# Norm factors in spare PSUM columns, a cross product read from the transform's bank, and a residual added on GpSimd, in the last phases of a two-layer kernel

## The chip, the cores and the metric

The kernel runs on one core of a Trainium2 chip. The metric is the device time of one execution in microseconds (us), the median of several runs. The engines are called here as the profile calls them: PE is the matmul engine (its weight loads are PEld), DVE is VectorE, ACT is ScalarE, POOL is GpSimd, and SP is the engine whose queue issues the DMAs in this part. SBUF is the on-chip working memory, PSUM the memory that matmuls write.

## What is computed

There are two layers with residuals, `x = x + layer(group_norm(x))`. Layer 0, a state-space scan in four directions, takes most of the time and is not touched. Layer 1 is a Fourier neural operator with attention over time steps. Its attention is computed before the part that matters here, which is the reference's last lines:

```python
projd = _fno_layer(out, wP, wPs, bPs, (H, W))
attention = _inorm(projd + xa, norm_g[1], norm_b[1])
an = _inorm(attention, norm_g[2], norm_b[2])
m = _fno_layer(an, wM0, wM0s, bM0s, (H, W), (norm_g[3], norm_b[3]), act=True)
m = _fno_layer(m, wM1, wM1s, bM1s, (H, W), (norm_g[4], norm_b[4]), act=False)
output = _inorm(m, norm_g[5], norm_b[5]) + attention
```

`_inorm` subtracts an image's mean, and divides by its standard deviation. `_fno_layer` is a truncated Fourier transform, a product with complex weights, the transform back (this is normalized where `norm_gb` is given), plus a scaled copy of its input (the skip), and for M0 a GELU. There are 192 images (4 x 48) of 128 x 48 points, in float32.

## The kernel before

The last part of `layer1` works on two strands, one for each pair of batches (`class Strand`, `p` is 0 or 1). A strand holds 96 images side by side (P = 96). An image tensor is laid out as 128 partitions (the long axis) by 48 rows by 96 images; `self.y` is the attention output in `xa`, `self.m` the MLP image. A block is 4 rows (QB), 128 x 384 elements, and fills 384 of the 512 columns of a PSUM bank.

A strand runs six phases. Each is a main generator (`p0` to `p5`) and a tail (`t0` to `t5`): `p0` and `t0` transform the projection back along the rows, `p1` along the columns, with sums for the norm of y and the forward transform for M0 beside it; `t1` makes the factors of that norm. `p2` multiplies by M0's weights and transforms back along the rows, `t2` makes the factor `t3` of M0's norm, `p3` transforms back along the columns, adds the skip, applies GELU, and starts M1's forward transform. `t3_` finishes that. `p4` and `t4` do for M1 what `p2` and `t2` do for M0, and make the factors `qe` and `qm` and a bias. `p5` and `t5` finish and store the output.

The loop at the end of `layer1` takes the phases of both strands in turn: p0 of strand 0, p0 of strand 1, p1 of strand 0, and so on. Beside each main generator it advances the tail of the phase before it, two steps of the tail for each step of the main. So `t2` of strand 0 is recorded beside `p2` of strand 1, and `p5` of strand 0 beside `t4` of strand 1. Instructions recorded through `on` keep their recorded order on their engine, so that an instruction waits behind all that were recorded before it. DMAs through `nc.sync` may be placed by the scheduler, and each engine and SP's queue then runs in order.

The lines that the change and the steps of the prediction touch:

- `rsqrt` writes a square root with ACT into a small SBUF vector of 128 x 96, and takes the reciprocal of it with DVE in place. `times` is an ACT copy with a scale.
- `open_sums` takes a new PSUM tile `st` for a strand's sums at the start of p1 to p4; each strand's tile has one bank. `sums` fills columns 0 to 383 of it; `total` reduces these with DVE and adds across partitions with PE.
- `p2` has POOL compute `m = y * sw` beside it, six blocks of 128 x 768 for each strand. `p3` has POOL scale `y` by `s1` in place, six more for each strand.
- `t2` ends with `t3 = t3 * s2`, a DVE product of two SBUF vectors. `p3` multiplies each loaded spectrum block `e2` (128 x 768) by `t3`.
- `along_h`, used by p0, p2 and p4, multiplies with PE into a bank, copies the bank to the SBUF tile `e` with ACT, and for each second bank calls `more`, and writes `e` to DRAM; `load_e2` loads it again with the axes turned (four DMAs for each block).
- `product` squares `e` with ACT or, in p4, also multiplies it with `a2`, on DVE, both from SBUF (`ce1`, 96 x 768). `beside` in p4 loads the layer's input `xr` and has POOL add it to `y`, six blocks of 128 x 768 for each strand.
- `p5` has for each second step a DVE product `e2 * qe` (called grade below), and `skip`: for two blocks of 128 x 768 each `m = m * qm`, then `m = m + y`, all on DVE with SBUF operands. Each step then adds two PSUM banks to `m` on DVE. `put` transposes finished rows with PE, adds the bias with ACT, and stores by DMA; step t puts the rows of step t - 1.

Of the kernel before, what the change touches and what calls it, by code (L numbers as in the profile page):

```python
# [10 lines left out]
F32 = mybir.dt.float32  # L11
BF16 = mybir.dt.bfloat16
AF = mybir.ActivationFunctionType
# [968 lines left out]
def layer1(ctx, tc, io, x1_dram, out):  # L982
# [893 lines left out]
    class Strand:  # L1876


        def __init__(self, p):
            self.p = p  # L1880
            self.y = xa[:, :, p * P : p * P + P]
            self.m = None
            self.e2 = {}

        def bank(self, name):
            return psum.tile([128, 512], F32, tag="mm", name=f"{name}_{self.p}")

        def open_sums(self, name):
            self.st = psst.tile([128, 512], F32, tag=f"st{self.p}", name=f"st_{name}_{self.p}")

        def blk(self, tag, shape, name, bufs):
            return work.tile(shape, F32, tag=tag, name=f"{name}_{self.p}", bufs=bufs)
# [19 lines left out]
            self.tot = [b[:, i * P : i * P + P] for i in range(len(mats))]  # L1912
            yield

        def rsqrt(self, name, v, bias, scale=1.0):
            r = self.vector(name)
            on.scalar.activation(r, v, AF.Sqrt, bias=bias, scale=scale)
            on.vector.reciprocal(r, r)
            return r

        def times(self, dst, src, factor):
            on.scalar.activation(dst, src, AF.Copy, scale=factor)
# [23 lines left out]
                yield  # L1946


        def along_h(self, name, fill, more=None, beside=None):
            self.de = dram.tile([2, H, 32, P], F32, name=f"de_{name}_{self.p}")  # L1950
            self.wait = []
            for k in range(0, 32, 4):
                if k % 8 == 0:
                    e = self.blk(f"spectra{self.p}", [128, 8, P], f"e_{name}{k}", 3)[0:96]
                b = self.bank(f"pe_{name}{k}")
                fill(b, k)
                if len(self.wait) > 1:
                    self.sums(self.wait.pop(0))
                on.scalar.copy(e[:, k % 8 : k % 8 + 4], images(b[0:96]))
                if k % 8 == 4:  # L1960
                    if more:
# [6 lines left out]
        def product(self, e, other, k0, name):  # L1968
            t = self.blk("ap", [128, 8, P], f"{name}{k0}", 4)[0:96]
            if other is None:  # L1970
                on.scalar.activation(t, e, AF.Square)
            else:
                on.vector.tensor_mul(t, e, other)
# [52 lines left out]

        def p1(self):

            self.open_sums("y")
            self.parts = []  # L2030
            for t in range(6):
                made = self.along_w("p", t, lambda h: pair_t[self.p][0:96, h])
                if t in (2, 4):
                    self.sums(self.parts[:4])
                    self.parts = self.parts[4:]
                for i, (b, h) in enumerate(made):
                    v = self.y[:, h : h + QB]
                    on.vector.tensor_add(v, v, images(b))
                    sq = self.blk("sq", [128, QB, P], f"sqy{h}", 4)
                    on.scalar.activation(sq, v, AF.Square)  # L2040
                    self.parts.append((2 * (t % 2) + i, one_m, sq, t < 2, t >= 4))
                if t:
                    self.forward("m0", self.y, t - 1, on.scalar.copy)
                yield
# [20 lines left out]
        def p2(self):  # L2065

            self.m = imgs.tile([128, H, P], F32, tag=f"p{self.p}", name=f"m_{self.p}")
            self.open_sums("m0")

            def fill(b, k):  # L2070
                for i in range(4):
                    on.tensor.matmul(b[0:96, i * P : i * P + P], sp_m[0][:, k + i], self.a2[:, k + i], start=True, stop=True)

            def more(e, k0):
                n = k0 // 8
                t = self.product(e, None, k0, "sqe0")
                self.wait.append([(2 * (n % 2) + i, one_s[0:96], t[i], n < 2, n >= 2) for i in range(2)])

            def beside(i):
                if i < 6:  # L2080
                    q = 8 * (3 * (i % 2) + i // 2)
                    on.gpsimd.tensor_mul(self.m[:, q : q + 8], self.y[:, q : q + 8], over(self.sw, 8))

            yield from self.along_h("m0", fill, more, beside)

        def t2(self):
            yield from self.load_e2("m0")
            for w in self.wait:
                self.sums(w)
            yield  # L2090
            yield from self.total((g_all,), "m0")
            on.vector.tensor_mul(self.s22, self.s22, self.tot[0])
            self.t3 = self.rsqrt("t3", self.s22, eps)
            on.vector.tensor_mul(self.t3, self.t3, self.s2)
            yield

        def p3(self):

            self.open_sums("g")
# [38 lines left out]

        def p4(self):

            self.open_sums("m1")

            def fill(b, k):
                for i in range(4):
                    on.tensor.matmul(b[0:96, i * P : i * P + P], sp_m[1][:, k + i], self.a2[:, k + i], start=True, stop=True)

            def more(e, k0):
                ts = [self.product(e, None, k0, "sqe1"), self.product(e, self.a2[:, k0 : k0 + 8], k0, "ce1")]
                self.wait.append(
                    [(2 * n + i, one_s[0:96], ts[n][i], k0 == 0, k0 == 24) for n in range(2) for i in range(2)]  # L2150
                )
# [7 lines left out]
                    v = self.y[:, q : q + 8]  # L2159
                    on.gpsimd.tensor_add(v, v, xr)  # L2160

            yield from self.along_h("m1", fill, more, beside)

        def t4(self):
            yield from self.load_e2("m1")
# [5 lines left out]
            t4 = self.rsqrt("t4", v4, eps)  # L2171
            self.times(t4, t4, n_g[:, 4:5])
            yield
            v5, u = self.vector("v5"), self.vector("d")
            on.vector.tensor_mul(v5, t4, v4)
            on.vector.tensor_mul(u, t4, cv)
            on.vector.tensor_mul(v5, v5, t4)
            self.times(u, u, w2)
            on.vector.tensor_add(v5, v5, self.vm)
            on.vector.tensor_add(v5, v5, u)  # L2180
            s5 = self.rsqrt("s5", v5, eps)
            self.times(s5, s5, n_g[:, 5:6])
# [3 lines left out]
            on.vector.tensor_mul(self.qe, t4, s5)  # L2186
            on.vector.tensor_mul(self.mu, self.mu, self.qm)
            yield
            b = self.bank("pbias")
# [54 lines left out]
    def images(b):  # L2244
        return b[:, 0 : QB * P].rearrange("p (a t) -> p a t", t=P)
# [123 lines left out]
```

## Time and profile before

The median of three runs is 4452.84 us (4444.05 to 4453.03). The execution that was profiled took 4458.8 us, with a span of 4457.0 us from its first to its last instruction.

| stretch of the span, us | what runs there | PE | DVE | ACT | POOL | PE clock | DMA share |
|---|---|---|---|---|---|---|---|
| whole span, 4457.0 | | 3808.3 | 3865.2 | 3440.9 | 3351.2 | 0.947 | |
| 4271 to 4290 | end of t1, p2 of both strands, t2 of strand 0 | 15.53 | 2.34 | 14.97 | 18.88 | 0.73 | 0.64 |
| 4290 to 4314 | t2 of strand 0 to the start of p3 | 2.67 | 23.93 | 4.29 | 23.60 | 0.63 | 0.28 |
| 4314 to 4339 | p3 of strand 0 | 17.31 | 11.68 | 14.74 | 0.00 | 0.74 | 0.25 |
| 4339 to 4361 | p3 of strand 1 | 16.84 | 11.41 | 13.87 | 0.00 | 0.92 | 0.47 |
| 4361 to 4400 | p4 of both strands, t4 of strand 0 | 31.77 | 14.92 | 21.46 | 16.62 | 0.67 | 0.97 |
| 4400 to 4432 | p5 of strand 0, t4 of strand 1 | 17.98 | 26.83 | 9.21 | 6.69 | 0.71 | 0.56 |
| 4432 to 4457 | p5 of strand 1 and the last stores | 15.61 | 19.04 | 9.08 | 0.00 | 0.84 | 0.36 |

The columns of engines are busy time in us within the stretch; the PE clock is the granted share of the full clock, and the DMA share is the mean busy share of the core's 16 DMA engines. A line of the timeline below gives the start in us, the duration in us, the engine, the line of the kernel (L55 is the helper through which all recorded operations pass, so operations are told apart by their tiles), the operation, output and inputs with their shapes, and in brackets the idle time before it and what ended it. An instruction that has been issued and is held within the engine counts as busy.

### The profile page before, as it was taken

To read this page: it belongs to the slowest core of one execution; us is meant where nothing else is said; L and a number is where in the kernel's file an instruction comes from. 1 tells how busy PE (TensorE), PEld (TensorE's weight loads), DVE (VectorE), ACT (ScalarE), POOL (GpSimd) and SP (SyncE) were. 2 spreads that over 40 slices of the span, in tenths; PEclk is the share of its full clock that TensorE was granted. 3 is DMA by queue.
4 is the path that set the end of the run, shared out by engine and by line. 5 is a ranking of instruction groups with operands and counts; after the bars stand their busy time and mean duration, and the time that the engine had idled before them with its cause. 6 is when DMAs were issued, how large, how long until landed. Compare 5 with 4: busy or idle time off the path is not lost. (4 is left out here: it accounts for less than half of the span.)

```text
span 4457.0 us, 73318 instructions
## 1 busy us (share of the span) xinstructions
PE 3808.3 (85%) x26040; PEld 2932.0 (66%) x26040; DVE 3865.2 (87%) x2652; ACT 3440.9 (77%) x6963; POOL 3351.2 (75%) x3515
## 2 busy tenths in 40 slices
PE   6989987888899978898999788878887796989866
PEld 3767776777677767776777677766776673534434
DVE  3989899999898999998999999998999995578546
ACT  3888888998788889987888898888999883424344
POOL 2777788988787889887778898887888984258432
PEclk9999999999899999998999999999999998999987
DMA  2333333433333333333333334334333333147536
GB/s 62 92 97 100 96 94 102 115 100 107 97 102 94 94 103 107 107 106 97 102 96 98 100 113 122 108 102 102 104 107 100 107 99 100 51 108 170 131 100 163
DMA packets 327946, 463.13 MB, mean 104 GB/s; under 512 B 112772, under 2 KB 295492, under 8 KB 326876
## 3 DMA queue, kind: packets, MB, share of 16 engines
q1 hardware_dynamic: 313072, 435.81, 35.7%
q10 hardware_dynamic: 14508, 22.64, 1.5%
q8 instruction: 206, 3.38, 0.3%
q14 instruction: 160, 1.31, 0.1%
HBM read 403.10 MB, written 55.44 MB: 103 GB/s over the span
## 5 line engine op out<-in xcount | busy, mean ns | idle before, releaser
L55 POOL TENSOR_TENSOR hc<-h,cbc 128x960 f32<-128x960 f32 (+1 forms) x1280 | 2546.4, 1991 | 563.0 <-PE yp L55 184.0
L55 DVE TENSOR_TENSOR_SCAN h<-da,carry,db 128x962 f32<-128x962 f32 (+1 forms) x640 | 1358.2, 2122 | 114.9 <-ACT da L55 95.5
L55 DVE TENSOR_TENSOR_SCAN h<-decay,carry,da 128x962 f32<-128x962 f32 (+1 forms) x640 | 1365.2, 2133 | 7.0 <-PE da L55 5.5
L55 PE MATMUL yp<-ident,hc 128*128 128x128 f32 (+1 forms) x9728 | 1263.2, 282 | 57.0 <-POOL hc L55 53.4
L55 PEld LDWEIGHTS yp<-ident,hc 128*128 128x128 f32 (+1 forms) x9728 | 1133.6, 144 | 222.8 <-issue 110.2
L55 ACT ACTIVATE scaled<-turned,bt 128x256 f32<-128x256 f32 (+1 forms) x2432 | 1037.2, 499 | 28.3 <-ACT turned L55 23.6
L55 ACT ACTIVATE da<-dt,a_neg 128x480 f32<-128x480 f32 (+1 forms) x1280 | 826.9, 646 | 187.3 <-DVE h L55 164.5
L55 ACT ACTIVATE decay<-dt,a_neg 128x480 f32<-128x480 f32 (+1 forms) x1280 | 800.2, 675 | 28.4 <-DVE h L55 23.9
L55 PE MATMUL da<-ident,scaled 128*128 128x128 f32 (+1 forms) x4864 | 647.2, 276 | 196.4 <-DVE h L55 180.8
L55 DVE TENSOR_TENSOR db<-du,pb 128x960 f32<-128x960 f32 (+1 forms) x640 | 701.3, 1096 | 110.4 <-PE pb L55 100.6
L55 PEld LDWEIGHTS da<-ident,scaled 128*128 128x128 f32 (+1 forms) x4864 | 544.3, 145 | 245.6 <-ACT scaled L55 100.0
L55 PE MATMUL pb<-ident,bt 128*128 128x128 f32 (+1 forms) x2432 | 375.7, 276 | 37.2 <-DVE db L55 37.1
L55 PEld LDWEIGHTS pb<-ident,bt 128*128 128x128 f32 (+1 forms) x2432 | 292.2, 141 | 169.3 <-issue 98.9
L55 PE MATMUL pc<-pad,w_c 128*128 128x480 f32 (+1 forms) x720 | 336.5, 582 | 6.5 <-ACT th L55 3.0
L55 POOL TENSOR_TENSOR du<-dt,xc 128x480 f32<-128x480 f32 (+1 forms) x160 | 206.3, 1290 | 49.9 <-ACT dt L55 49.9
L1769 PE MATMUL acc<-v,attn_c 128*64 128x384 f32 x1152 | 203.0, 492 | 9.1 <-DVE v L1751 5.4
L55 PEld LDWEIGHTS da<-carry,ident 128*128 128x128 f32 x1280 | 201.6, 199 | 0.0
L55 PE MATMUL da<-carry,ident 128*128 128x2 f32 x1280 | 197.7, 224 | 0.0
L55 POOL COPY carry<-h 128x2 f32<-128x2 f32 x1024 | 194.3, 190 | 0.0
L1753 POOL TENSOR_TENSOR v<-grep,xrep 128x768 f32<-128x768 f32 x88 | 162.7, 1852 | 35.1 <-PE acc L1769 23.3
L55 PE MATMUL pd<-xd,w_dt 40*128 40x480 f32 (+1 forms) x320 | 172.1, 619 | 16.7 <-ACT bt L55 7.8
L1751 DVE TENSOR_TENSOR v<-gp,xrep 128x1536 f32<-128x1536 f32 x88 | 153.7, 1754 | 27.6 <-PE acc L1769 12.4
(395 smaller groups left out, 3863.5 us busy)
## 6 DMA issues: line engine op xcount, KB each, us to landing
cbc<-cd SPq DMA_DIRECT2D x512, 240.0 KB
cbc<-other SPq DMA_DIRECT2D x512, 240.0 KB
xrep<-dxt SPq DMA_DIRECT2D x44, 576.0 KB
cbc<-cd SPq DMA_DIRECT2D x128, 192.0 KB
cbc<-other SPq DMA_DIRECT2D x128, 192.0 KB
yt<-turned ACTq DMA_DIRECT2D x40, 384.0 KB
old<-yt SPq DMA_DIRECT2D x40, 384.0 KB
grep<-dgt SPq DMA_DIRECT2D x16, 576.0 KB
```

Of the source, the lines that this page charges most:

```text
L55: return lambda *args, **kw: self._tc.keep_in_program_order(emit(*args, **kw))
L1751: nc.vector.tensor_mul(v, gp[:, None, :, 0:NC].to_broadcast([128, 2, 2, NC]), x[:, :, 0:2])
L1753: nc.gpsimd.tensor_mul(v3, r[:, 2:3].to_broadcast([128, 2, NC]), x[:, :, 2])
L1769: nc.tensor.matmul(acc[c][64 * b : 64 * b + 64, 0:NC], attn_c[:, 2 * pair + b, g, q], v[:, b, c] if c < 2 else v3[:, b], start=first, stop ...
```

## The change

Four things change, all in the last phases of the second layer.

1. Each strand takes one `st` tile for good, and a vector `tv` in its columns 384 to 479, which the sums leave free. `rsqrt` may write its reciprocal to a given place. `t3`, and later `v5`, `s5` and `qm`, lie in `tv`; `qe` stays in SBUF.
2. In p4 the cross product is made bank by bank: `each`, called after ACT's copy of a bank, multiplies the PSUM bank with `a2` (96 x 384). The product from `e` in SBUF (96 x 768) goes.
3. In p5 `skip` only multiplies by `qm`. The residual `y` is added block by block (128 x 384) after the bank: on POOL for steps 0 to 4, on DVE for step 5.
4. In p5 the grades and skips are recorded earlier, and `put` runs two steps behind rather than one.

```diff
+            self.st = psst.tile([128, 512], F32, tag=f"st{p}", name=f"st_{p}")
+            self.tv = self.st[:, QB * P : QB * P + P]
...
-        def rsqrt(self, name, v, bias, scale=1.0):
+        def rsqrt(self, name, v, bias, scale=1.0, to=None):
             r = self.vector(name)
             on.scalar.activation(r, v, AF.Sqrt, bias=bias, scale=scale)
-            on.vector.reciprocal(r, r)
-            return r
+            to = r if to is None else to
+            on.vector.reciprocal(to, r)
+            return to
...
-            self.t3 = self.rsqrt("t3", self.s22, eps)
+            self.t3 = self.rsqrt("t3", self.s22, eps, to=self.tv)
             on.vector.tensor_mul(self.t3, self.t3, self.s2)
...
                 on.scalar.copy(e[:, k % 8 : k % 8 + 4], images(b[0:96]))
+                if each:
+                    each(b, k)
...
+            def each(b, k):
+                k0, j = 8 * (k // 8), k % 8
+                if j == 0:
+                    cross[k0] = self.blk("ap", [128, 8, P], f"ce1{k0}", 4)[0:96]
+                v = cross[k0][:, j : j + 4]
+                on.vector.tensor_mul(v, images(b[0:96]), self.a2[:, k : k + 4])
...
-            v5, u = self.vector("v5"), self.vector("d")
+            v5, u = self.tv, self.vector("d")
...
-            s5 = self.rsqrt("s5", v5, eps)
+            s5 = self.rsqrt("s5", v5, eps, to=self.tv)
...
-            self.qe, self.qm = self.vector("t3"), self.vector("sw")
+            self.qe, self.qm = self.vector("t3"), self.tv
...
+            def grade(q):
+                on.vector.tensor_mul(self.e2[q], self.e2[q], over(self.qe, 8))
+
             def skip(q):
                 for i in range(2):
                     v = self.m[:, 24 * i + q : 24 * i + q + 8]
                     on.vector.tensor_mul(v, v, over(self.qm, 8))
-                    on.vector.tensor_add(v, v, self.y[:, 24 * i + q : 24 * i + q + 8])
-
+
+            grade(0)
+            skip(0)
             for t in range(6):
-                q = 8 * (t // 2)
-                if t % 2 == 0:
-                    on.vector.tensor_mul(self.e2[q], self.e2[q], over(self.qe, 8))
-                    skip(q)
-                for b, h in self.along_w("m1", t):
+                made = self.along_w("m1", t)
+                if t == 1:
+                    grade(16)
+                    skip(8)
+                if t == 3:
+                    skip(16)
+                for b, h in made:
                     v = self.m[:, h : h + QB]
                     on.vector.tensor_add(v, v, images(b))
-                if t:
-                    self.put(t - 1)
+                    add = on.vector if t == 5 else on.gpsimd
+                    add.tensor_add(v, v, self.y[:, h : h + QB])
+                if t == 0:
+                    grade(8)
+                if t > 1:
+                    self.put(t - 2)
                 yield
+            self.put(4)
```

More of the change, by code (lines that the diff above doesn't have):

```diff
@@ L1883, in __init__ @@
             self.e2 = {}
+            self.st = psst.tile([128, 512], F32, tag=f"st{p}", name=f"st_{p}")
+            self.tv = self.st[:, QB * P : QB * P + P]
         def bank(self, name):
             return psum.tile([128, 512], F32, tag="mm", name=f"{name}_{self.p}")
-        def open_sums(self, name):
-            self.st = psst.tile([128, 512], F32, tag=f"st{self.p}", name=f"st_{name}_{self.p}")
         def blk(self, tag, shape, name, bufs):
@@ L1946, in load_a2, with along_h @@
                 yield
-        def along_h(self, name, fill, more=None, beside=None):
+        def along_h(self, name, fill, more=None, beside=None, each=None):
             self.de = dram.tile([2, H, 32, P], F32, name=f"de_{name}_{self.p}")
@@ L1966, in along_h, with product @@
                 yield
-        def product(self, e, other, k0, name):
+        def product(self, e, k0, name):
             t = self.blk("ap", [128, 8, P], f"{name}{k0}", 4)[0:96]
[L1970 to L1973, printed above, removed]
+            on.scalar.activation(t, e, AF.Square)
             if k0 == 0:
@@ L2027, in p1 @@
         def p1(self):
-            self.open_sums("y")
             self.parts = []
@@ L2067, in p2 @@
             self.m = imgs.tile([128, H, P], F32, tag=f"p{self.p}", name=f"m_{self.p}")
-            self.open_sums("m0")
             def fill(b, k):
@@ L2075, in more @@
                 n = k0 // 8
-                t = self.product(e, None, k0, "sqe0")
+                t = self.product(e, k0, "sqe0")
                 self.wait.append([(2 * (n % 2) + i, one_s[0:96], t[i], n < 2, n >= 2) for i in range(2)])
@@ L2097, in p3 @@
         def p3(self):
-            self.open_sums("g")
             self.parts = []
@@ L2139, in p4 @@
         def p4(self):
-            self.open_sums("m1")
             def fill(b, k):
@@ L2145, in fill @@
                     on.tensor.matmul(b[0:96, i * P : i * P + P], sp_m[1][:, k + i], self.a2[:, k + i], start=True, stop=True)
+            cross = {}
+            def each(b, k):
[4 more added lines that the diff above has]
+                on.vector.tensor_mul(v, images(b[0:96]), self.a2[:, k : k + 4])
+                if k == 0:
+                    self.times(v[:, 0], v[:, 0], first_k)
             def more(e, k0):
-                ts = [self.product(e, None, k0, "sqe1"), self.product(e, self.a2[:, k0 : k0 + 8], k0, "ce1")]
+                ts = [self.product(e, k0, "sqe1"), [cross[k0][:, 4 * i : 4 * i + 4] for i in range(2)]]
                 self.wait.append(
@@ L2160, in beside @@
                     on.gpsimd.tensor_add(v, v, xr)
-            yield from self.along_h("m1", fill, more, beside)
+            yield from self.along_h("m1", fill, more, beside, each)
         def t4(self):
@@ L2180, in t4 @@
             on.vector.tensor_add(v5, v5, u)
-            s5 = self.rsqrt("s5", v5, eps)
+            s5 = self.rsqrt("s5", v5, eps, to=self.tv)
             self.times(s5, s5, n_g[:, 5:6])
             yield
-            self.qe, self.qm = self.vector("t3"), self.vector("sw")
+            self.qe, self.qm = self.vector("t3"), self.tv
+            on.vector.tensor_mul(self.qe, t4, s5)
             self.times(self.qm, s5, wsm[1])
-            on.vector.tensor_mul(self.qe, t4, s5)
             on.vector.tensor_mul(self.mu, self.mu, self.qm)
```

## The prediction

> **What bounds the kernel now.** The change touches only what follows the second layer's attention, so I first read the busy times by stretch. From 4290 to 4314 us DVE is busy 23.93 of 24 us, in three instructions, with PE at 2.67 and ACT at 4.29. DVE's timeline shows which instruction, and POOL's what ran beside it:
>
> ```profile
> 4288.11 0.26 DVE L55 TENSOR_TENSOR s<-s,tot_m 128x96 f32<-128x96 f32 x1 [0.55 <-PE tot_m L55]
> 4289.84 0.75 DVE L55 RECIPROCAL t<-t 128x96 f32<-128x96 f32 x1 [1.47 <-ACT t L55]
> 4290.63 23.09 DVE L55 TENSOR_TENSOR t<-t,s 128x96 f32<-128x96 f32 x1
> 4313.75 0.96 DVE L55 TENSOR_TENSOR e_m<-e_m,t 128x768 f32<-128x768 f32 x1
> ```
> ```profile
> 4285.30 7.18 POOL L55 TENSOR_TENSOR m<-xa,sw 128x768 f32<-128x768 f32 x4
> 4292.43 21.17 POOL L55 TENSOR_TENSOR xa<-xa,s 128x768 f32<-128x768 f32 x12
> ```
>
> The product `t3 * s2` takes 23.09 us; for strand 1, with POOL idle, it takes 0.26 (at 4337.63). It ends at 4313.72, when POOL's unbroken run ends (4292.43 + 21.17 = 4313.60): DVE was held until POOL fell silent, over 13 POOL instructions. The two DVE instructions before it ran beside the same POOL run at 0.26 and 0.75 us: one has a PSUM input (`tot_m`), the other only one input. So only DVE products of **two SBUF inputs** are held. The chain of waits agrees: it has 23.10 us on `DVE t`.
>
> In p5 of strand 0 the same happens on a small scale, while POOL adds `xr`:
>
> ```profile
> 4401.50 0.94 DVE L55 TENSOR_TENSOR m<-m,sw 128x768 f32<-128x768 f32 x1
> 4402.55 2.47 DVE L55 TENSOR_TENSOR m<-m,xa 128x768 f32<-128x768 f32 x1
> 4404.94 2.55 DVE L55 TENSOR_TENSOR m<-m,sw 128x768 f32<-128x768 f32 x1
> 4407.60 0.96 DVE L55 TENSOR_TENSOR m<-m,xa 128x768 f32<-128x768 f32 x1
> ```
> ```profile
> 4402.40 4.28 POOL L55 TENSOR_TENSOR xa<-xa,xr 128x768 f32<-128x768 f32 x2 [2.51 <-DMA xr<-x]
> ```
>
> Here the engines alternate, since POOL's second add waits for a DMA. Apart from these holds p5 is bound by DVE (26.83 of 32 us, then 19.04 of 25, and the chain is mostly `DVE m`), and p4 by PE (31.77 of 39 us) at a low clock, with the DMA engines 0.97 busy beside it.
>
> **The held product: -20.4 us.** After the change the product reads `tv` in PSUM and `s2` in SBUF, so it should take 0.26 us and end at 4290.9. The next grade by `t3` needs its spectrum loaded; SP issues those twelve loads from 4288.72, the fourth at about 4291.5. In p1 the last of the first four loads was issued at about 4211.4 and used at 4212.73, so the first block lands at about 4293.3, as late as DVE is then: 4313.75 - 4293.3 = 20.4. Bounds: 22.8 if the load is never late, 14.7 if it waits until the DMA engines fall idle (4299). POOL stays busy until 4313.6, but in the order of the changed kernel each DVE product up to then (`e_m * st`, `m + pi_m`) has a PSUM operand, and POOL's rows of `m` for strand 0 are six products from 4271.12, so done by 4282. Layer 0 has that pair at full speed for millisecond after millisecond:
>
> ```profile
> L55 POOL TENSOR_TENSOR hc<-h,cbc 128x960 f32<-128x960 f32 (+1 forms) x1280 | 2546.4, 1991 | 563.0 <-PE yp L55 184.0
> L55 DVE TENSOR_TENSOR db<-du,pb 128x960 f32<-128x960 f32 (+1 forms) x640 | 701.3, 1096 | 110.4 <-PE pb L55 100.6
> ```
>
> DVE's `db` has one SBUF and one PSUM input, and takes 1.1 us for 960 columns beside POOL. That DVE writes a PSUM vector is in no row of DVE here; ACT reads one at 0.34 us against 0.38 for SBUF, so I take it at no cost, with 0 to 0.5 us as bounds for the seven small operations on the path.
>
> [...]
>
> **The cold clock: -2.5 us.** In the stall PE sits idle 22.1 us, and the clock is halved when p3 starts:
>
> ```profile
> 4316.00:4319.00 3.00, 1.83 (x6) 0.49 (x3) 2.28 (x5) 1.81 (x4) 0.00 (x0) 0.50 0.00 0
> 4319.00:4322.00 3.00, 2.27 (x6) 0.92 (x8) 0.63 (x1) 2.78 (x5) 0.00 (x0) 0.50 0.00 0
> 4349.00:4352.00 3.00, 3.00 (x26) 0.81 (x24) 1.73 (x4) 1.82 (x4) 0.00 (x0) 1.00 0.03 7
> ```
>
> (after the width: busy PE, PEld, DVE, ACT, POOL; then the clock, 0.50 and later 1.00). Afterwards the gap is 1.6 us, and after an idle 1.7 us at 4352.5 the clock was still 1.00. The first PE groups (3.02 + 1.74 + 1.55 + 1.1 = 7.4 us) take 4.5 at the full clock (3 x 0.92 + 0.87 + 0.85). Following the order by hand, the fourth pair of bank adds, 13.0 us after the first grade (4326.78), begins 10.3 after it: 2.7. I take 2.5, bounds 0 and 2.9. The rest of p3 and p4 then shifts as a whole.
>
> **p4 and t4: -1.0 us.** The reduction for strand 1 (at 4369.96) now stands behind the first half of the third cross product, which needs ACT's copy ending at 4370.24: +0.9, with PE waiting. DVE's sixteen half products cost 0.47 each against 0.87 for a whole, 0.5 us more in all, hidden where DVE is busy 14.92 of 39 us. In t4 of strand 0 the add `v + d` took 1.67 us beside a POOL add; with `v` in PSUM it takes 0.26: -1.4. Half products instead of whole ones ahead of `v` and of the first grade of p5: -0.4 and -0.5. Against that, the first grade (two SBUF inputs) then falls into a POOL add of `xr`, and may be held for up to 1.6. Bounds +1.2 to -2.3; I take -1.0.
>
> **p5 of strand 0, up to the first grade of strand 1: -5.0 us.** Before, this took 4400.63 to 4431.81, 31.2 us. DVE loses six adds of `y` (128x768, 0.96 each, 5.8) and the two holds (1.5 + 1.6), and gains two adds of 128x384 (0.95): 8.0 less. It now ends by the chain through POOL: the adds of `y` queue behind the last add of `xr`, which ended 9.6 us in. A POOL add of 384 columns lies between 0.90 (half of the 1.80 for 768) and 1.10 (the 384-column form of `du`); I take 0.95, as operands and tiles are those of `xr`. From about 9 us the six adds of steps 0 to 2 end at 14.5 to 15; PE, which keeps its order, does the transposes of step 0, banks of step 3, transposes of step 1, banks of step 4, transposes of step 2 (1.1 and 0.9 us each) and only then `tot_m` of t4, at about 20. Then ACT, DVE and the four-step factor chain, 6.5 us as before (4425.25 to 4431.81): 26.2, so -5.0. The grades are held once or twice by `xr` adds within this, which the POOL chain covers. Bounds: -9 (only DVE counts) and +2 (POOL at 1.10, each put waiting).
>
> **p5 of strand 1 and the end: -1.6 us.** Before, 25.2 us (4431.81 to 4457.0): 19.9 on DVE, 5.3 for the last transposes, ACT and store. DVE's own sum is now 3 x 0.87 + 6 x 0.87 + 12 x 0.47 + 2 x 0.47 = 14.4; two grades held by the POOL adds of step 0 add 1.4, and the banks of step 5, behind three transposes that wait for POOL, and its last adds of `y`, held by POOL's adds of steps 3 and 4, bring it to 18.2. With 5.4 for the end: 23.6. Bounds -5 and +3.
>
> [...]
>
> **The sum.** 20.4 + 2.5 + 1.0 + 5.0 + 1.6 = 30.5 us. Against the profiled execution (4458.8) that is 4428.3; the median shown is 6 us lower, so I forecast 4452.8 - 30.5 = **4422 us**. About 0.2%, 8.9 us, is what a measurement can tell from no change; the three runs alone spread over 9.
>
> **Rivals.**
> - *POOL paces p5.* The adds of `y` stand behind those of `xr`, a put waits for them, and PE's `tot_m` for the put; grades wait for whole POOL runs. For: the 23 us hold. Against: 10 short adds with gaps. The last two terms then give nothing: 4452.8 - 23.9 = 4429. Chance 0.21.
> - *DVE alone paces p5.* The last two terms reach -9 and -5: 4415 or less. For: DVE is the bound there now. Chance 0.13.
> - *The hold stays.* If a PSUM operand doesn't free the product, the first two terms go, and 7.6 us remain: 4445. Against: `s<-s,tot_m` and `db`. Chance 0.04.
> - *Slower: POOL's adds of 384 columns are long.* All 20 lie one after another on the path to the puts, so each us above 0.95 costs 20 us. Against the 23.9 us of the first terms and the 8.9 of the bound, the kernel is slower from 0.95 + 1.64 = 2.6 us for each; at 3.0 it would be 4452.8 - 23.9 + 41 = 4470. Against: 1.10 is the longest row of this size. Chance 0.03.
> - My forecast: 0.59.
>
> The range must hold the two p5 rivals, the bounds of the load (5.7 us) and the scatter of the runs (-9 to 0): **4408 to 4437**. Faster by over 0.2%: 0.93; within: 0.04; slower: 0.03.
>
> **What would show it.** In the profile after: `st<-st,s` at 0.3 us beside POOL; first grade of p3 within 3 us of it; clock 1.00 in p3; `v + d` near 0.26; POOL's 128x384 adds near 0.95, and what PE waits for ahead of `tot_m`. Wrong would be a hold on another DVE instruction before POOL's run ends, or p3 starting later because its load lands late.

## The result, and the profile after

The changed kernel takes 4430.79 us (median of 11 runs, 4415.32 to 4440.38) against 4450.03 us before (median of 11, 4437.48 to 4463.06) on the same chip: a ratio of 0.9956, 95% interval 0.9941 to 0.9971, so 13 to 26 us faster. The forecast was 4422 with a range of 4408 to 4437.

The profiled execution took 4425.95 us (span 4424.2). The 14 profiles of this study reach the last part of layer 1 at times that differ by 27 us, through code that no edit touches. So stages are compared from one common event, **POOL's first product `m<-xa,sw`** in p2 (4271.12 us before, 4258.94 after), and all "from zero" numbers below count from there.

DVE's and POOL's timelines of the changed kernel, where the hold was (start, duration, engine, operation, idle before it):

```profile
4277.94 0.26 DVE L55 TENSOR_TENSOR s<-s,tot_m 128x96 f32<-128x96 f32 x1 [1.36 <-PE tot_m L55]
4280.00 0.76 DVE L55 RECIPROCAL st<-t 128x96 f32<-128x96 f32 x1 [1.80 <-ACT t L55]
4280.80 0.27 DVE L55 TENSOR_TENSOR st<-st,s 128x96 f32<-128x96 f32 x1
4283.42 0.96 DVE L55 TENSOR_TENSOR e_m<-e_m,st 128x768 f32<-128x768 f32 x1 [2.36 <-DMA e_m<-de_m]
4288.05 1.02 DVE L55 TENSOR_TENSOR m<-m,pi_m 128x384 f32<-128x384 f32 x2 [3.68 <-PE pi_m L55]
```
```profile
4258.94 21.36 POOL L55 TENSOR_TENSOR m<-xa,sw 128x768 f32<-128x768 f32 x12 [75.45 <-ACT sw L55]
4280.25 21.31 POOL L55 TENSOR_TENSOR xa<-xa,s 128x768 f32<-128x768 f32 x12
```

POOL's run is as long as before and lies at the same place; the product `st<-st,s` takes 0.27 us in the midst of it. The grade behind it now waits 2.36 us for its load, and the first bank adds wait 3.68 us for PE, where they waited 1.82 before:

```profile
4316.53 1.02 DVE L55 TENSOR_TENSOR m<-m,pi_m 128x384 f32<-128x384 f32 x2 [1.82 <-PE pi_m L55]
```

That is the new thing. The next lines are whole stretches of both kernels, from the end of PE's wait for strand 1's first DMA in p2 until PE is next idle (after the width: busy PE, PEld, DVE, ACT, POOL; then the clock):

```profile
4270.38:4289.23 18.85, 18.85 (x90) 12.71 (x90) 3.82 (x7) 9.68 (x17) 18.85 (x12) 0.50 0.65 169
```
```profile
4282.20:4292.67 10.47, 10.47 (x82) 8.14 (x82) 3.61 (x4) 7.05 (x14) 10.47 (x7) 0.83 0.63 171
```

The first is the changed kernel, the second the kernel before: strand 1's rest of p2 takes PE 10.47 us where the clock comes back to 1.00 on the way. Where it stays at 0.50 it takes 15.9 (to 4286.30), and p3's first eight transforms behind it the rest of the 18.85. In t4 of strand 0, one add took 1.67 us (first line, the kernel before); now all are short:

```profile
4393.00 1.67 DVE L55 TENSOR_TENSOR v<-v,d 128x96 f32<-128x96 f32 x1
```
```profile
4365.76 0.26 DVE L55 TENSOR_TENSOR st<-st,t 128x96 f32<-128x96 f32 x1
4366.05 0.27 DVE L55 TENSOR_TENSOR st<-st,vm 128x96 f32<-128x96 f32 x1
4366.42 0.27 DVE L55 TENSOR_TENSOR st<-st,d 128x96 f32<-128x96 f32 x1
```

In p5 of strand 0, POOL's and PE's timelines after:

```profile
4381.82 1.81 POOL L55 TENSOR_TENSOR xa<-xa,xr 128x768 f32<-128x768 f32 x1 [1.57 <-DMA xr<-x]
4383.58 5.77 POOL L55 TENSOR_TENSOR m<-m,xa 128x384 f32<-128x384 f32 x6
4390.37 1.96 POOL L55 TENSOR_TENSOR m<-m,xa 128x384 f32<-128x384 f32 x2 [1.02 <-DVE m L55]
```
```profile
4384.64 2.05 PE L55 MATMUL pf<-ident,m 128*96 128x128 f32 x8 [4.21 <-POOL m L55]
...
4392.27 1.08 PE L55 MATMUL pf<-ident,m 128*96 128x128 f32 x8
4393.19 0.58 PE L55 MATMUL tot_m<-red,g 128*128 128x96 f32 x4
```

POOL's adds of `y` take 0.96 us each and start when the last `xr` is added, at 4383.63; the first transposes (`pf`) wait 4.21 us for them, and `tot_m` of strand 1 comes behind the third group of transposes, at 4393.19.

All profiles by stage, in us. "Grade" is a strand's first product of a spectrum by `t3` in p3, "vm" strand 0's variance in t3_; p5 of strand 0 runs from its first grade to that of strand 1.

| kernel | first grade p3, from zero | strand 1's grade, from zero | vm, from zero | vm to p5's first grade | p5 strand 0 | p5 strand 1, to the end | end, from zero | ratio to before, 95% interval |
|---|---|---|---|---|---|---|---|---|
| before | 42.63 | 68.08 | 93.31 | 36.20 | 31.18 | 25.19 | 185.88 | 1 |
| changed | 24.48 | 52.37 | 78.49 | 34.83 | 28.85 | 23.09 | 165.26 | 0.9956 (0.9941 to 0.9971) |
| changed, second profile | 24.59 | 50.61 | 76.46 | 35.07 | 28.44 | 23.01 | 162.98 | |
| t3_only | 23.24 | 50.53 | 76.42 | 36.05 | 31.54 | 25.21 | 169.22 | 0.9960 (0.9946 to 0.9974) |
| t3_back | 42.64 | 68.83 | 95.04 | 34.87 | 28.89 | 23.10 | 181.90 | 0.9984 (0.9969 to 0.9999) |
| run_cut | 32.10 | 57.55 | 83.44 | 41.83 | 32.68 | 25.17 | 183.12 | 1.0009 (0.9995 to 1.0024) |
| run_broken | 43.08 | 68.61 | 95.05 | 31.42 | 33.31 | 25.19 | 184.97 | 1.0005 (0.9989 to 1.0021) |
| before_warm | 42.76 | 68.20 | 94.10 | 36.69 | 31.16 | 25.49 | 187.44 | |
| warm | 21.16 | 43.33 | 69.13 | 35.12 | 28.83 | 24.24 | 157.32 | 0.9924 (0.9905 to 0.9943) |
| xr_p3 | 23.96 | 51.93 | 78.01 | 34.17 | 23.65 | 24.51 | 160.34 | 0.9937 (0.9916 to 0.9959) |
| qe_psum | 24.28 | 50.61 | 76.33 | 35.19 | 28.24 | 21.67 | 161.43 | 0.9930 (0.9907 to 0.9953) |
| y_dve | 24.69 | 52.35 | 78.47 | 34.84 | 29.94 | 26.01 | 169.26 | 0.9951 (0.9931 to 0.9970) |
| cross_back | 24.48 | 50.58 | 76.39 | 34.67 | 28.98 | 23.12 | 163.16 | |
| all_three | 21.68 | 44.61 | 69.61 | 36.38 | 21.47 | 21.86 | 149.32 | 0.9914 (0.9895 to 0.9933) |

Each ratio is to runs of the kernel before that were taken beside that kernel's. The ratios' intervals are 0.3 to 0.5% wide, so a difference of a few us is read from the stages, not from the times.

### The profile page after: what moved, and what is told of

The parts are those of the page before. It is cut to its first block, busy times and chain, and to the rows that moved or that the text cites. A ratio compares the mean times of both kernels' runs of the same rounds, so it can differ in the third digit from the quotient of the medians.

```text
span 4424.2 us, 73361 instructions
## 1 busy us (share of the span) xinstructions
PE 3803.3 (86%) x26040; PEld 2924.4 (66%) x26040; DVE 3834.4 (87%) x2652; ACT 3436.8 (78%) x6963; POOL 3368.5 (76%) x3535
## 5 line engine op out<-in xcount | busy, mean ns | idle before, releaser
L55 ACT ACTIVATE scaled<-turned,bt 128x256 f32<-128x256 f32 (+1 forms) x2432 | 1035.5, 497 | 29.1 <-ACT turned L55 22.7
L55 ACT ACTIVATE decay<-dt,a_neg 128x480 f32<-128x480 f32 (+1 forms) x1280 | 799.2, 674 | 28.4 <-DVE h L55 23.6
L1753 POOL TENSOR_TENSOR v<-grep,xrep 128x768 f32<-128x768 f32 x88 | 162.4, 1848 | 35.8 <-PE acc L1769 22.9
```

Source lines behind the costliest of these rows:

```text
L55: return lambda *args, **kw: self._tc.keep_in_program_order(emit(*args, **kw))
L1753: nc.gpsimd.tensor_mul(v3, r[:, 2:3].to_broadcast([128, 2, NC]), x[:, :, 2])
```

## The experiments

The theory: a DVE product of two SBUF operands is held by POOL's run, one PSUM operand frees it, and that is most of the gain; the rest is p5's. The main rival: the product ended with POOL's run for another reason, and p5's new order is what gains.

### One part of the change alone, and all but that part

**t3_only** is the kernel before with a persistent `st` bank and the factor in it:

```diff
-            self.t3 = self.rsqrt("t3", self.s22, eps)
+            self.t3 = self.rsqrt("t3", self.s22, eps, to=self.tv)
```

> The kernel before with one part of the change alone: the sums' bank of each strand stays the same tile through all phases, and the factor t3 (with its product by s2) lies in that bank's free columns. Cross product, t4 and p5 are as before. Theory (a DVE product of two SBUF operands is held until GpSimd's unbroken run ends, and one PSUM operand frees it): the product t3*s2 of strand 0 takes 0.27 us in place of 23.09, the first grade of p3 begins 4 to 6 us after the product s22*tot_m (25.6 before), the first grade of strand 1 in p3 comes 15 to 19 us earlier counted from GpSimd's first product of m, p5 keeps its 31.2 + 25.2 us, and the kernel is 15 to 19 us faster than before. Rival (the product waits for something else that ends with GpSimd's run, or the load is as late anyway): the first grade moves by under 3 us and the kernel by under 4.

**t3_back** is the changed kernel with that line reverted.

> The changed kernel with t3 back in SBUF; everything else of the change stays. Theory: the hold of about 23 us returns on t3*s2 of strand 0, and the kernel loses 15 to 19 us of the change's 19, so that it stands 2 to 6 us under the kernel before; what is left is the part of the cross product, of t4 and of p5. Rival (p5's rearrangement carries a good part of the gain): it stays 9 us or more faster than before.

DVE's timelines of t3_only and of t3_back:

```profile
4274.33 0.27 DVE L55 TENSOR_TENSOR st<-st,s 128x96 f32<-128x96 f32 x1
4276.22 0.95 DVE L55 TENSOR_TENSOR e_m<-e_m,st 128x768 f32<-128x768 f32 x1 [1.62 <-DMA e_m<-de_m]
```
```profile
4283.84 20.97 DVE L55 TENSOR_TENSOR t<-t,s 128x96 f32<-128x96 f32 x1
4304.84 0.96 DVE L55 TENSOR_TENSOR e_m<-e_m,t 128x768 f32<-128x768 f32 x1
```

The one line decides whether the product takes 0.27 or 21 us. t3_only ends 16.7 us earlier from zero than before, t3_back 4.0; together 20.7, and the whole change has 20.6 in one profile and 22.9 in the other. So the parts add up within the scatter of a profile (that they meet to 0.1 us is luck), and some three quarters or four fifths of the gain are that line. The rest lies in p4 and p5: t3_back has them as short as the changed kernel (34.87, 28.89 and 23.10 us), t3_only as long as before (36.05, 31.54 and 25.21). By the times t3_only alone cannot be told from the whole change.

### How long the hold lasts

**run_cut** (the kernel before) makes POOL's run six products shorter:

```diff
-                on.gpsimd.tensor_mul(v, v, over(self.s1, 8))
+                if self.p == 0:
+                    on.gpsimd.tensor_mul(v, v, over(self.s1, 8))
...
+                    if self.p:
+                        on.gpsimd.tensor_mul(v, v, over(self.s1, 8))
                     on.gpsimd.tensor_add(v, v, xr)
```

> The kernel before, with GpSimd's six products of strand 1's y by s1 moved out of p3 to p4 of strand 1, each just ahead of the addition of xr to the same rows; nothing is left out. GpSimd's unbroken run beside t3*s2 is then six products (10.6 us) shorter. Theory (DVE is held until the run ends): t3*s2 takes 12 to 13 us in place of 23.09 and ends with the run; the first grade of p3 comes about 10.5 us earlier, and the kernel is 7 to 11 us faster than before. Rival (the hold is as long as one GpSimd instruction, and the product ended at 4313.7 for another reason): t3*s2 keeps about 23 us.

```profile
4289.88 10.57 DVE L55 TENSOR_TENSOR t<-t,s 128x96 f32<-128x96 f32 x1
4300.48 0.96 DVE L55 TENSOR_TENSOR e_m<-e_m,t 128x768 f32<-128x768 f32 x1
```
```profile
4289.66 10.68 POOL L55 TENSOR_TENSOR xa<-xa,s 128x768 f32<-128x768 f32 x6
```

The hold ends with the run again (4300.45 against 4300.34), so its length is POOL's. The kernel, though, was not 7 to 11 us faster: 10.5 us at the first grade are 2.8 at the end, and none in the times. Strand 1's products now fill POOL's gaps in p4, and the small products of strand 0's t4 run into them, each held for about one POOL instruction:

```profile
4380.52 1.52 DVE L55 TENSOR_TENSOR v<-v,t 128x96 f32<-128x96 f32 x1
4382.08 1.84 DVE L55 TENSOR_TENSOR v<-v,vm 128x96 f32<-128x96 f32 x1
4384.03 1.67 DVE L55 TENSOR_TENSOR v<-v,d 128x96 f32<-128x96 f32 x1
```

From vm to p5's first grade it takes 41.83 us in place of 36.20: 5.6 us of the gain were given back there, and 1.5 more in p5 of strand 0. The first two lines account for 2.85 us of it (these products took 0.25 and 0.26 before); what makes the rest is not shown, and PE's clock was lower there too (0.58 against 0.64).

**run_broken** (the kernel before) puts a POOL instruction that reads no SBUF behind each product:

```diff
                 on.gpsimd.tensor_mul(v, v, over(self.s1, 8))
+                on.gpsimd.memset(gap, 0.0)
```

> The kernel before, with a GpSimd memset of one column of an unread tile behind each of its twelve products y*s1; nothing is left out, no operand moves to PSUM. Until now every hold of some length stood beside a run of equal GpSimd products without any gap, while beside GpSimd's additions, which wait for DMAs or for DVE, a DVE product came in after one instruction. Theory A (DVE comes in wherever GpSimd stops reading SBUF, be it for one short instruction): t3*s2 takes at most 2 us in place of 23.09, the first grade of p3 comes 15 to 19 us earlier, and the kernel is 14 to 19 us faster than before. Theory B (DVE waits until GpSimd has no instruction ready at all): t3*s2 takes 23 to 26 us, and the kernel is as before or up to 3 us slower.

```profile
4294.05 1.82 POOL L55 TENSOR_TENSOR xa<-xa,s 128x768 f32<-128x768 f32 x1
4295.80 0.12 POOL L55 MEMSET gap<- 128x1 f32 x1
4295.86 1.83 POOL L55 TENSOR_TENSOR xa<-xa,s 128x768 f32<-128x768 f32 x1
```
```profile
4294.55 21.23 DVE L55 TENSOR_TENSOR t<-t,s 128x96 f32<-128x96 f32 x1
```

Theory B: the product still waits to 4315.78, past twelve memsets (the last began at 4315.60). It is not enough that POOL stops reading for 0.1 us between two instructions.

### The clock

**same_again** is the changed kernel unaltered.

> The changed kernel once more, unaltered, for a second profile of it. In the first, PE's clock fell to 0.50 4.5 us after GpSimd's first product of m and came back 37.5 us after it, though PE was busy without a gap from 11.4 to 30.3; before, it came back after 14.4 us with the same instructions. If that is chance of the execution, this profile may show another length, and the first grade of p3 and the fourth pair of bank adds come earlier by up to 2 and 5 us when it is short. If the change causes it (the rival), the clock comes back at 37 to 38 us again.

Inside the slow stretch, and where the clock had come back:

```profile
4264.80:4285.10 20.30, 18.13 (x90) 12.74 (x90) 3.25 (x6) 11.00 (x22) 20.30 (x12) 0.50 0.71 181
4285.40:4288.40 3.00, 0.98 (x6) 0.42 (x4) 2.09 (x4) 2.92 (x6) 3.00 (x3) 1.00 0.01 3
```

The clock was at 0.50 from 8.9 to 29.4 us from zero, not from 4.4 to 38.5 as in the first profile (the expectation put that end at 37.5). So its length is chance of the execution. It takes two forms in the seven profiles where the product is free and no unread products run: it came back at 38.0 to 38.5 us in three (changed, xr_p3, y_dve; strand 1's grade at 51.9 to 52.4) and first at 29.1 to 29.4 in four (same_again, t3_only, qe_psum, cross_back; 50.5 to 50.6). The first grade came at 24.59 all the same (it waits for its load, 2.76 us), strand 1's at 50.61 in place of 52.37.

**warm** keeps PE busy in two gaps of p2 of the changed kernel (`keep_busy(n)` issues n products of 128x384 into a bank that nothing reads):

```diff
+                if name == "m0" and k == 0 and self.p == 1:
+                    self.keep_busy(6)
                 fill(b, k)
+                if name == "m0" and k == 16 and self.p == 0:
+                    self.keep_busy(4)
```

> The changed kernel, with ten matrix products into an unread bank put into two idle gaps of PE in p2: four after strand 0's fifth bank (PE waits 2.31 us for ACT's squares there) and six ahead of strand 1's first (PE waits 1.5 to 3.7 us for a DMA). They change no output. Theory (with the clock at 0.50 strand 1's rest of p2 keeps PE busy for 18.6 us, 10.5 at full clock as before, and p3's first inverse transforms queue behind it, which is what the forecast's clock term missed): the clock is 1.00 from GpSimd's first product of m to the first grade of p3, the first bank adds come within 3 us of that grade in place of 4.2 to 4.6, the first grade itself at 21 to 23 us in place of 24.5, and strand 1's first grade in p3 3 to 6 us earlier than 50.6 to 52.4. Rival (the clock's gap is hidden, by the load of the spectra or by ACT): strand 1's first grade in p3 stays at 50 to 52.

**before_warm** is the same edit on the kernel before.

> The kernel before, with the same ten unread matrix products in p2 that gained 8 to 9 us on the changed kernel up to the end of p3. Theory (the hold covered the slow clock: it ends with GpSimd's run, whatever PE's clock does meanwhile): the clock is 1.00 in p2's rest, but t3*s2 still ends with GpSimd's run and the first grade of p3 stays at 42.6 us from GpSimd's first product of m, and strand 1's first grade at 66 to 69. Rival (the clock costs the same with and without the hold): both come 6 to 9 us earlier.

The stretches of warm around the rest of p2 and the start of p3, and DVE there:

```profile
4266.00:4286.00 20.00, 19.26 (x136) 12.64 (x136) 3.76 (x7) 15.54 (x34) 20.00 (x13) 1.00 0.78 202
4286.00:4296.00 10.00, 7.26 (x48) 2.74 (x48) 5.35 (x11) 8.87 (x14) 10.00 (x6) 1.00 0.38 109
```
```profile
4283.22 0.27 DVE L55 TENSOR_TENSOR st<-st,s 128x96 f32<-128x96 f32 x1
4285.44 0.95 DVE L55 TENSOR_TENSOR e_m<-e_m,st 128x768 f32<-128x768 f32 x1 [1.95 <-DMA e_m<-de_m]
4287.48 1.95 DVE L55 TENSOR_TENSOR m<-m,pi_m 128x384 f32<-128x384 f32 x4 [1.09 <-PE pi_m L55]
```

And of before_warm, the rest of p2, then the hold:

```profile
4256.00:4276.00 20.00, 19.23 (x136) 12.61 (x135) 5.74 (x6) 15.53 (x34) 20.00 (x13) 1.00 0.75 189
4276.00:4297.00 21.00, 0.00 (x0) 0.00 (x0) 20.98 (x1) 1.90 (x2) 20.86 (x12) 0.52 0.23 65
```
```profile
4273.19 23.79 DVE L55 TENSOR_TENSOR t<-t,s 128x96 f32<-128x96 f32 x1
4297.02 0.96 DVE L55 TENSOR_TENSOR e_m<-e_m,t 128x768 f32<-128x768 f32 x1
```

At a clock of 1.00 the changed kernel has its first grade 3.3 us and strand 1's 7 to 9 us earlier, more than the 3 to 6 expected, and keeps it to vm. Its end comes 6 to 8 us earlier from zero. Of the kernel before, the same edit moves neither grade by 0.2 us: the product starts earlier and is held longer. In t3_back, where the clock stood at 0.50 from 3.8 to 55 us from zero, the first grade is at 42.64 too. The hold was the cover of the slow clock, and when it went, the clock became what is late next.

### p5

**xr_p3** moves the loads and adds of `xr`, for both strands, to p3 of the changed kernel:

```diff
                 on.gpsimd.tensor_mul(v, v, over(self.s1, 8))
+                xr = self.blk("xr", [128, 8, P], f"xr{r}", 2)
+                for b in range(2):
+                    nc.sync.dma_start(xr[:, :, b * T : (b + 1) * T], x1_dram[2 * self.p + b][:, r : r + 8])
+                on.gpsimd.tensor_add(v, v, xr)
...
-            yield from self.along_h("m1", fill, more, beside, each)
+            yield from self.along_h("m1", fill, more, None, each)
```

> The changed kernel, with the loads of xr and GpSimd's additions of xr to y moved from p4 to p3 of the same strand, each right behind the product y*s1 of the same rows; nothing is left out. In the two profiles of the changed kernel the last addition of xr ends 11.2 us after p5's first grade, and p5 of strand 0 takes 28.4 to 28.9 us where 26.2 were forecast from additions that end at 9. Theory (that last addition sets when GpSimd's adds of y, the puts, and PE's tot_m behind them begin): with xr added 60 us earlier, p5 of strand 0 takes 23 to 26 us, p4 loses some waits for DMA too, and the kernel is 4 to 9 us faster than the changed one. Rival 1 (DVE sets p5): p5 of strand 0 stays at 28 us. Rival 2: the loads stand ahead of p3's own transfers on SP's queue, p3 grows by 4 us or more, and the kernel is no faster.

POOL's adds of `y` in p5 of strand 0, whose first grade is at 4370.94:

```profile
4374.28 2.66 POOL L55 TENSOR_TENSOR m<-m,xa 128x384 f32<-128x384 f32 x2 [33.20 <-DVE m L55]
4380.03 5.77 POOL L55 TENSOR_TENSOR m<-m,xa 128x384 f32<-128x384 f32 x6 [3.09 <-DVE m L55]
```

They begin 3.3 us in, and wait for DVE; p5 of strand 0 takes 23.65 us in place of 28.4 to 28.9, as the theory has it. PE's clock was higher there too (0.79 against 0.68), and its part in the 5 us is not separated. From vm to p5's first grade it takes 0.7 to 0.9 us less, and p3 is as long as in the changed kernel's two profiles (vm at 78.01, between 76.46 and 78.49), so rival 2 falls. Strand 1's p5 lost 1.4 (PE's clock was 0.78 there, 0.87 in the changed kernel); why is not shown. The end comes 2.6 to 4.9 us earlier from zero; the times' intervals overlap with those of the changed kernel.

**qe_psum** frees the grades as well:

```diff
-            self.qe, self.qm = self.vector("t3"), self.tv
+            self.qe, self.qm = self.st[:, 0:P], self.tv
```

> The changed kernel with the factor qe in PSUM too, in the first 96 columns of the strand's sums' bank, which are free once the last sums are reduced. The three grades of p5 then have one SBUF operand. Theory (grades of two SBUF operands are held by GpSimd's additions beside them): each grade takes 0.96 us; for strand 0 the three took 1.83 + 4.38 us and for strand 1 0.96 + 3.25, so DVE gets back 3.3 and 1.3 us. p5 of strand 1 gets 1 to 1.5 us shorter (23.1 to 21.8); p5 of strand 0 under 1 us, as GpSimd's additions set its end there. Rival (DVE sets p5 of strand 0 too): that gets 3 us shorter as well. Kernel 1 to 5 us faster than the changed one.

The second and third grades of strand 1, first in the changed kernel, then here:

```profile
4404.74 3.25 DVE L55 TENSOR_TENSOR e_m<-e_m,t 128x768 f32<-128x768 f32 x2
```
```profile
4391.16 1.81 DVE L55 TENSOR_TENSOR e_m<-e_m,st 128x768 f32<-128x768 f32 x2
```

As expected: 1.4 us in p5 of strand 1 and 0.2 to 0.6 in that of strand 0, though DVE was held for over 3 us there.

**y_dve** leaves POOL out of p5:

```diff
-                    add = on.vector if t == 5 else on.gpsimd
-                    add.tensor_add(v, v, self.y[:, h : h + QB])
+                    on.vector.tensor_add(v, v, self.y[:, h : h + QB])
```

> The changed kernel, with DVE doing all additions of y in p5, none on GpSimd; order and puts as changed. DVE has 20 more additions of 128x384 (0.47 us each, 9.4 in all), GpSimd nothing in p5 but the last additions of xr. Theory (GpSimd's chain, not DVE, sets p5 of strand 0): p5 of strand 0 takes 26 to 29 us, as before or less, and p5 of strand 1, which ends on DVE, 24 to 25.5 in place of 23.1. Rival (DVE sets both): 32 to 33 and 27 to 28 us, and the kernel is 8 us slower than the changed one.

p5 of both strands, in y_dve:

```profile
4386.85:4416.79 29.94, 17.65 (x86) 9.94 (x86) 27.09 (x44) 8.25 (x17) 7.80 (x4) 0.71 0.62 163
4416.79:4442.80 26.01, 17.88 (x80) 9.94 (x80) 20.26 (x33) 10.00 (x16) 0.00 (x0) 0.85 0.41 122
```

29.94 and 26.01 us lie between the two theories: POOL's adds gain 1.1 to 1.5 us for strand 0 and 2.9 for strand 1. They are all that p5 gained: without them p5 of both takes 55.95 us, against 56.4 before.

**cross_back** takes the cross product from ACT's copy again, in blocks of 96x768.

> The changed kernel with the cross product of p4 as before: one product of 128x768 form (96x768) from ACT's copy in SBUF for two banks, in place of two half products from the banks. Theory (p4 waits on PE and DMAs, and DVE's halves lie in its idle time): from strand 0's vm to p5's first grade 34.8 to 35.6 us, against 34.8 and 35.1 for the changed kernel and 36.2 before; the 1.1 to 1.4 gained against before are those of v in PSUM and of the halves ahead of the first grade in about equal parts. Rival (the bank as source is what gains): 36 us or more.

34.67 us, no more than the changed kernel's 34.83 and 35.07: here the bank as source gained nothing. But in this profile no cross product was held, all eight took 0.95 to 1.03 us. In t3_only, whose p4 and t4 are those of the kernel before, POOL's adds of `xr` lay otherwise, and it was the cross products (two SBUF inputs) that were held, while `v + d` was not:

```profile
4354.75 2.24 DVE L55 TENSOR_TENSOR ce<-e_m,a_m 96x768 f32<-96x768 f32 x1 [0.80 <-ACT e_m L55]
4357.88 0.26 DVE L55 TENSOR_TENSOR v<-v,d 128x96 f32<-128x96 f32 x1
4363.10 2.42 DVE L55 TENSOR_TENSOR ce<-e_m,a_m 96x768 f32<-96x768 f32 x1 [2.67 <-DMA e_m<-de_m]
```

The stretch took 36.05 us there, 36.20 before. So which product is held depends on when an `xr` lands; in the changed kernel none of the sixteen halves took over 0.56. How the 1.1 to 1.4 us of p4 and t4 divide between the bank and t4's operands in PSUM is not shown.

### A version with all of it

**all_three** joins the edits of warm, xr_p3 and qe_psum.

> The changed kernel with all three gains together: the ten unread products that keep PE's clock up in p2, the loads and additions of xr moved to p3, and qe in PSUM. Theory (they lie in different stages and add up): strand 1's first grade in p3 at 42 to 45 us from GpSimd's first product of m, p5 of strand 0 22.5 to 24 us, of strand 1 21.5 to 23.5, the end at 148 to 153 where the changed kernel has 163 and 165; 10 to 15 us faster than the changed kernel, ratio to before 0.990 to 0.993. Rival (they share a cover, such as the loads in p3 that now collide with faster PE work): the end at 156 or later.

The end lies at 149.32 us from zero, 14 to 16 before the changed kernel's, and the ratio to before is 0.9914 (0.9895 to 0.9933; medians 4415.09 and 4450.81): its interval lies wholly below the changed kernel's. It is faster than both the changed kernel and the one before, though p4 took 1.3 to 1.6 us more than in the changed kernel.

## Why the prediction was right, and where its steps were not

Counted from zero, the change gained 20.6 us in the first profile and 22.9 in the second; the times say 19.2. The sum was 30.5. What it rests on, that one operand in PSUM frees the product, came true; about half of the 8 to 10 us that were missing lie in one step, the cold clock.

- **The held product, -20.4: right in mechanism, 2.3 us short counted from zero.** From `s<-s,tot_m` to the first grade it took 25.64 us before and 5.48 after: 20.2. Counted from zero it is 18.1, since that instruction itself came 2.0 us later, PE's sums and `tot_m` running at a clock of 0.50. The grade waited 2.36 us for its load; the forecast had 2.4 (4293.3 - 4290.9). One reading beside it was wrong: that the engines alternate in p5 "since POOL's second add waits for a DMA". The wait of 2.51 us in that row is ahead of its first add; the second follows without a gap (at 4404.16), and DVE's `m<-m,xa`, held since 4402.55, got in between the two.
- **The cold clock, -2.5: the step that failed.** It laid the halved clock to the stall alone, and took it to be 1.00 once the stall was gone; in the profile of before it was at 1.00 from 14.7 to 24.9 us from zero, up to the stall. That was the exception: in the ten other profiles without the unread products it fell to 0.50 by 8.9 us from zero and stayed there to 29.1 at least. Strand 1's rest of p2, 15.9 us of PE at that clock, now stands in front of p3's first transforms; before, it ran beside the hold. From the first grade to strand 1's it took 27.89 and 26.02 us against 25.45: +2.4 and +0.6 in place of -2.5, and 0.6 to 0.9 more to vm (the kernels with the hold spread from 25.2 to 26.4 there, so that may be scatter). With the clock kept up (warm) strand 1's grade comes 24.8 us earlier than before, where these two steps had 22.9 together. The text itself wrote that the rest of p3 "shifts as a whole"; what it missed was the work of the other strand in PE's queue. No bound of the range covered a loss here (the term's bounds were 0 and 2.9); the measured time lies in the range only because that was wide enough for its other terms, in this respect by luck.
- **p4 and t4, -1.0: right as a sum** (-1.4 and -1.1, and -1.3 in t3_back). PE's clock was no higher there (0.61 against 0.64). Of its parts, `v + d` took 0.27 as forecast; what the cross product from the bank gave is not shown (cross_back, t3_only).
- **p5 of strand 0, -5.0: it was -2.3 and -2.7.** The chain through POOL was right, two of its times were not. The last `xr` was added 11.4 and 11.0 us in, not at 9, since its loads come by DMA and kept their own time (46.2 and 46.1 us behind vm, 45.8 before) while p5 began earlier; `tot_m` came at 20.9 and 20.5, forecast about 20. From there to strand 1's grade it took 7.9, where the sum had 6.5. Half of that is the forecast's own count: it took its 6.5 from 4425.25, 0.7 behind the start of `tot_m` (4424.56). The other 0.7 came with the new order, which puts ACT's copies of `pf`, and DVE's two adds of `y` of step 5, among t4's small operations. In xr_p3, without the wait for `xr`, it is 23.65 us.
- **p5 of strand 1, -1.6: -2.1 and -2.2,** right.
- POOL's adds of 384 columns took 0.96 us, forecast 0.95; a PSUM operand cost DVE nothing (0.27 against 0.26 us for the product by `s2`; in the kernel before 0.245 for `v<-t,tot_m`, which reads PSUM, against 0.250 for `v<-v,t`).

The measured 4431 is near the 4429 of the rival "POOL paces p5", but not by its way: POOL does pace p5 of strand 0, yet p5 gained 4.4 to 4.9 us as a whole. Of the 9.9 and 7.6 us that were missing, 8.1 and 6.0 lie ahead of vm, where PE's clock was slow, and 2.7 and 2.3 in p5 of strand 0.

How long a product was held differed: in t3_back, before_warm and run_broken 21 to 24 us, twelve POOL products and more; the three products of run_cut's t4 above, and the two of p5 in the kernel before, were held for 1.3 to 1.6 us, about one POOL instruction (1.8 us). Nor did the clock come back at one time behind PE's last idle time: in the kernel before it came back at about 4285.8, 3.6 us after it; in the changed one PE was busy for 18.85 us by the profile, and the clock stayed at 0.50.

## What to carry to other kernels

A small product on the critical path with two SBUF operands is worth moving to PSUM, if only one operand of it, when GpSimd runs a row of products beside it: here it took 0.27 us in place of 23.09, and 20.97 with the operand back in SBUF (t3_back). Before a stall is counted as a gain, list what the other engines work off behind it, the other strand's work too, and at which clock; a single profile does not tell the clock (in the changed kernel it came back at 38.5 us from zero in one profile, at 29.4 in the other), so give that term a bound from both sides. Cheap unread matmuls in PE's short waits brought the end 6 to 8 us forward here, and loads moved to where the DMA engines were less busy (a share of 0.41 in the changed kernel from p3's first grade to vm, 1.00 from vm to p5's first grade) 3 to 5; all the finer edits of the change together brought 4 (t3_back).

## What the runs showed of the hardware

- The hold's length differs by what POOL runs. Beside rows of six to thirteen products with a broadcast factor it lasted to the end of the row (10.57 to 23.79 us), also with memsets between them; beside adds of two full operands DVE came in after one instruction, even where eight adds ran without a gap (`m<-m,xa` on DVE took 1.06 us in place of 0.56). In run_cut, where products and adds take turns, it came in behind a product too (`v<-v,t`, 1.52 us). Whether the broadcast operand, the wait that an add carries, or the size decides stays open.
- Busy time does not tell the clock. In p4 of the changed kernel PE was busy 23.96 us of 27 (4345 to 4372), and the clock stood at 0.50 throughout; in the second profile it was 24.05 of 27 (4340 to 4367), at 0.50 again.
- A single idle time of PE does not tell it either. After one of 2.31 us in p2 the clock fell in the first profile of the changed kernel and stayed at 1.00 in the second, to fall 5.6 us later within an idle time of 3.69 us; in warm it stayed at 1.00 past idle times of 0.59, 1.24 and 2.25 us, to the end of strand 0's p3. What decides is not shown.
- In the 14 profiles, from zero to 60 us behind it, each stretch at one clock that begins and ends there lasts a whole multiple of 3.41 us (3.4, 6.8, 10.2, 13.7 and so on, up to 51.2).
- What PE's clock does in p4 can outweigh what the change does there, by one profile: run_broken has p4 of the kernel before, and took 31.42 us from vm to p5's first grade at a mean clock of 0.92, where the kernel before took 36.20 at 0.64. Part of it was lost again: p5 of strand 0 took 33.31 us in place of 31.18, with the last `xr` added 15.1 us in, not 9.6.
